# The head of a two-layer graph kernel: the attention weights' product moved to the front of the projections

## The chip, the cores and the metric

The kernel runs on one core of one Trainium2 chip. The time is device microseconds of one execution, as the median of several runs; a profile is one further execution, recorded by the hardware. The engines are TensorE (PE, with its weight load PEld), VectorE (DVE), ScalarE (ACT), GpSimd (POOL) and SyncE (SP, which here only issues DMAs). Each engine takes its instructions in program order and waits for others by semaphores.

## What is computed

Two layers over 4096 rows x of 512 numbers and a 4096 x 4096 matrix adj. Only the start of layer 0 matters here:

```
h = max(layernorm(x), 0)
q = h @ Wq.T + bq ;  k = h @ Wk.T + bk ;  v = h @ Wv.T + bv
x = x + softmax(q @ k.T / sqrt(512) + 2 * adj) @ v
# layer 1: a graph attention with 8 heads over the same rows, W, a1, a2, a_ln, b_ln
```

The kernel never forms k. Since q @ k.T is (h @ Wq.T + bq) @ (h @ Wk.T).T up to a term that is constant along a softmax row, it forms A = Wq.T @ Wk once (512 x 512) and a vector c from bq and Wk, and then "queries" h @ A + c, which are multiplied with h itself. All of it is in fp32.

## The kernel before

`fast_path` does everything (a general path follows for inputs that it can't take; it isn't run here). Its first part, the projections, is what the change touches. Rows come in eight blocks `sb` of 512. These steps exist for a block:

- `load_x(sb)` (L400): four DMAs of 128 rows, 256 KB each, on SP's queue.
- layernorm: `means`/`stats` (L176, L419) take mean and variance on DVE; an inverse root follows; then the rows are scaled and shifted in place. For block 0 `normalize` (L406) does roots and scaling on DVE; for the others `normalize_ahead` (L424) does the roots on POOL and the scaling on ACT (L433).
- `hidden(sb, xt)` (L438): 16 PE transposes (128 x 128) into four PSUM banks `pt`, four ACT relu copies into `hT` (L444), four POOL sums and differences of its quarters into `hS` (L452 to L455), and seven DMAs on SP that store both to DRAM.
- `values_of(sb, between)` (L517): h @ Wv.T + bv by seven half-size products in place of eight (a Strassen scheme, `seven`, L489). The products come in four stages; a stage's results go into PSUM banks named X and Z, two of each, and DVE adds each one into the result (L510, L520). A later product may accumulate on a bank that DVE has read. After each stage, `between` gives one piece of other work to put into the engines' queues. Four POOL differences for each pair of 128-row blocks (L531 to L534) and two stores end it.
- `queries(sb, between)` (L543): the same for h @ A + c. The result tile `qs` has one buffer; four POOL differences (L565 to L568) and seven stores to `q_d` follow.

`seven` needs differences of the quarters of a weight matrix; `weight_sums` (L462) makes them with four POOL instructions, for Wv and for A.

All instructions in this part are under `keep_in_program_order`, so the order in each engine's queue is the order of the code. Before the change it is: loads of x(0), Wv and x(1); loads of Wq and Wk in blocks of 32 columns with 512-byte rows (`load_blocks`, L329) and of Wk once more as whole rows (`wk_rows`); `normalize(x(0))`; Wv's sums; `hidden(0)`; `values_of(0)`, with block 1's statistics and scaling between its stages; four DVE transposes of Wq's 32 x 32 blocks (`turn_blocks`, L337); `hidden(1)`; a POOL multiply of Wk's rows with bq (L611); `values_of(1)` with Wk's four DVE transposes between its stages; c (L615); block 2's statistics and scaling; `attention_vectors` (L210, DVE, for layer 1); the product A (L623, 16 matmuls of 128 x 512 columns, each two PE instructions) and its four ACT copies out of PSUM (L627); A's sums; `queries(0)`; `hidden(2)`; `queries(1)`; then for each further block `values_of`, `hidden` of the next, `queries`. The small preparations for layer 1 (`aside`: constants, centred and weighted W) are cut into steps; `go_on` puts one step in, and stands between stages of `queries(0)` and of the later blocks.

The weights are kept for this time in parts of the big tile `v` whose own values come much later: blocks 8 to 11 and 16 to 31. The bias vectors and layer 1's vectors are loaded from ACT's queue after `hidden(0)`.

Of the kernel before, what the change touches and what calls it, by code (L numbers as in the profile page):

```python
# [10 lines left out]
F32 = mybir.dt.float32  # L11
# [7 lines left out]
P = 128  # L19
# [60 lines left out]
def fast_path(  # L80
# [95 lines left out]
    def means(pool, rows, name, mv=None, some=range(SB)):  # L176

        st = pool.tile([P, SB, 6], F32, name=f"{name}st", tag=f"{name}st", bufs=2)
        if mv is None:
            mv = pool.tile([P, SB, 2], F32, name=f"{name}mv", tag=f"{name}mv", bufs=2)  # L180
        for b in some:
            seq(nc.vector.bn_stats(st[:, b, :], rows[b]))
            seq(nc.vector.bn_aggr(mv[:, b, :], st[:, b, :]))
        return mv
# [11 lines left out]
    def over_heads(t):  # L196
        return t.unsqueeze(1).to_broadcast([P, NH, HD])
# [122 lines left out]
    with tc.tile_pool(name="rows_in", bufs=2) as rows_in, tc.tile_pool(  # L320
# [70 lines left out]
        with tc.tile_pool(name="proj_v", bufs=1) as pv, tc.tile_pool(  # L391
# [11 lines left out]
                    seq(nc.sync.dma_start(out=xt[:, b, :], in_=x[ts(sb * SB + b, P), :]))  # L403
                return xt

            def normalize(xt):  # L406
                mv = means(work, [xt[:, b, :] for b in range(SB)], "h")
                var = work.tile([P, SB], F32, name="hv", tag="hv", bufs=1)
                seq(nc.vector.tensor_scalar_add(var, mv[:, :, 1], LN_EPS))
                rstd = inverse_root(nc.vector, work, var, SB, "h")  # L410
                for b in range(SB):
                    seq(nc.vector.tensor_scalar(
                        xt[:, b, :], xt[:, b, :], mv[:, b, 0:1], rstd[:, b : b + 1],
                        ALU.subtract, ALU.mult,
                    ))

            mvs = {}

            def stats(sb, *blocks):  # L419
# [1 line left out]
                    mvs[sb] = work.tile([P, SB, 2], F32, name="hmv", tag="hmv", bufs=2)  # L421
                means(work, [xts[sb][:, b, :] for b in range(SB)], "h", mvs[sb], blocks)

            def normalize_ahead(sb):  # L424
                mv = mvs.pop(sb)
                var = work.tile([P, SB], F32, name="hv", tag="hv", bufs=1)
                seq(nc.gpsimd.tensor_scalar_add(var, mv[:, :, 1], LN_EPS))
                rstd = inverse_root(nc.gpsimd, work, var, SB, "h")
                shift = work.tile([P, SB], F32, name="hs", tag="hs", bufs=1)
                seq(nc.gpsimd.tensor_mul(shift, mv[:, :, 0], rstd))  # L430
                seq(nc.gpsimd.tensor_scalar_mul(shift, shift, -1.0))
                for b in range(SB):
                    seq(nc.scalar.activation(  # L433
                        xts[sb][:, b, :], xts[sb][:, b, :], AF.Identity,
                        scale=rstd[:, b : b + 1], bias=shift[:, b : b + 1],
                    ))

            def hidden(sb, xt):  # L438
                h, sums = hidden_tiles(sb)
# [134 lines left out]
            def room(first, blocks, m):  # L574
                return v[:, first : first + blocks, :].rearrange(
                    "p b d -> p (b d)"
                ).rearrange("p (m c) -> p m c", m=m)

            raw = {"q": room(16, KC, GC // R), "k": room(20, KC, GC // R)}
# [20 lines left out]
            def turn_weights(name, c):  # L600
                turn_blocks(turned[name][:, c, :], raw[name], c)

            def calls(f, *each):
                return [lambda a=a: f(*a) for a in each]
# [6 lines left out]
            seq(nc.gpsimd.tensor_mul(  # L611
                wk_rows, wk_rows, bq_sb.unsqueeze(1).to_broadcast([P, KC, D])
            ))
            values_of(1, calls(turn_weights, *(("k", c) for c in range(SB))))
            seq(nc.vector.tensor_reduce(c_sb, wk_rows, AX.X, ALU.add))  # L615
            seq(nc.vector.tensor_scalar_mul(c_sb, c_sb, half_scale))
            stats(2, *range(SB))
            normalize_ahead(2)
            attention_vectors(v[:, 15, :])
            for k in range(KC):  # L620
                pa_ps = psum.tile([P, 512], F32, name="pa", tag="XZ"[k % 2], bufs=2)
                for c in range(SB):
                    seq(nc.tensor.matmul(  # L623
                        pa_ps, turned["q"][:, c, ts(k, P)], turned["k"][:, c, :],
                        start=c == 0, stop=c == SB - 1,
                    ))
                seq(nc.scalar.activation(a_sb[:, k, :], pa_ps, AF.Identity, scale=half_scale))  # L627
# [1315 lines left out]
```

## Time and profile before

| | us |
|---|---|
| median of three runs (lowest, highest) | 3564.26 (3562.43, 3565.39) |
| the profiled execution's own time | 3564.05 |
| its span, first to last instruction | 3562.1 |
| PE busy in the span | 3496.1 (98%) |
| DVE, ACT, POOL busy | 2571.6, 1765.6, 2286.7 |
| PE's first instruction | 14.17 |
| first matmul of `values_of(2)` | 95.83 |
| first attention product (L715) | 250.35 |

The projections take the first 250 us. The busy times of a pipelined PE say that it had work, not that it ran at its best, so they are read beside the granted clock (1.00 is full speed). A wait in the views is written with the engine and line that released it: `[2.34 <-ACT a_sb L627]` means that the engine had been idle for 2.34 us until the instruction of line 627 on ACT was done.

### The profile page before, as it was taken

The page shows a single profiled execution, that of the slowest core. Times are in us where ns is not written, and L with a number is a line of the kernel's source. Part 1 is how long each engine was busy: PE and PEld are TensorE (multiplying, and loading weights), DVE is VectorE, ACT ScalarE, POOL GpSimd, SP SyncE. Part 2 cuts the span into 40 slices and gives each one's busy share as a digit, 9 for nine tenths or more (in the row PEclk, how much of TensorE's full clock was granted, in tenths as well). Part 3 has the DMA queues.
Part 4 walks back from the last instruction along what each step waited for, and adds up shares of the span by engine and source line. Part 5 has one row for each costly group of instructions (what it writes and reads, how often), then busy time and mean ns, then how long its engine had stood idle before and what let it go on. Part 6 is the DMA issues. An engine that isn't in the chain of part 4 may idle for free.

```text
span 3562.1 us, 59727 instructions
## 1 busy us (share of the span) xinstructions
PE 3496.1 (98%) x21866; PEld 2149.3 (60%) x21866; DVE 2571.6 (72%) x4268; ACT 1765.6 (50%) x1570; POOL 2286.7 (64%) x1857
## 2 busy tenths in 40 slices
PE   7999999999999999999999999999999999999998
PEld 5888888888888888888878222222322222232222
DVE  5666565656566665656557888888888888888887
ACT  1111111111111111111123899999999999999997
POOL 5664444454444454444456788888888888888886
PEclk9999999999999999999999999999999999999999
DMA  6687888888888788888758777787787777777775
GB/s 204 207 250 226 242 240 236 247 245 236 246 241 242 238 242 246 240 244 240 232 123 182 205 200 205 207 218 207 209 220 215 208 215 205 200 211 208 214 212 151
DMA packets 636958, 779.86 MB, mean 219 GB/s; under 512 B 78512, under 2 KB 465264, under 8 KB 627440
## 3 DMA queue, kind: packets, MB, share of 16 engines
q1 hardware_dynamic: 618800, 742.60, 72.4%
q0 software_dynamic: 16464, 31.98, 5.2%
q8 instruction: 174, 2.85, 0.3%
q10 hardware_dynamic: 1392, 1.38, 0.2%
q14 instruction: 128, 1.05, 0.1%
HBM read 593.76 MB, written 174.19 MB: 216 GB/s over the span
## 4 chain that ended last, share of the span: by engine, by line
PE 88%; DVE 7%; ACT 1%; DMA 1%; issue 1%; POOL 0%; SPq 0%; DVEq 0%; ACTq 0%; POOLq 0%
PE accs L1083 25%; PE XZ L715 21%; PE M L770 20%; PE r L1044 4%; PE r L1014 4%; PE l L1024 3%; PE X L503 3%; PE l L1044 3%; PE Z L503 2%; DVE t L1071 2%; PE y L1276 1%; PE pt L1147 1%; DVE x L826 1%; DVE y L1160 1%; PE accs L1276 1%
## 5 line engine op out<-in xcount | busy, mean ns | idle before, releaser
L1068 POOL TENSOR_TENSOR t<-t,g 128x1024 f32<-128x1024 f32 x512 | 1224.7, 2400 | 272.7 <-DVE t L1062 236.5
L1083 PE MATMUL accs<-t,nX 128*64 128x512 f32 x4096 | 1003.0, 605 | 4.7 <-DVE ob L1137 4.7
L1075 ACT ACTIVATE t<-t 128x2048 f32<-128x2048 f32 (+1 forms) x527 | 976.3, 1853 | 0.2 <-POOL t L1068 0.2
L1062 DVE SCALAR_TENSOR_TENSOR t<-u,at2m,r 128x512 f32<-128x512 f32 x1024 | 719.3, 744 | 193.8 <-issue 151.7
L731 ACT ACTIVATE aT<-aT 128x512 f32<-128x512 f32 x256 | 161.2, 630 | 1388.6 <-DVE aT L727 1388.6
L727 DVE TENSOR_TENSOR aT<-aT,XZ 128x256 f32<-128x256 f32 x891 | 351.5, 418 | 580.6 <-PE XZ L715 576.2
L1071 DVE TENSOR_TENSOR t<-l,g 128x1024 f32<-128x1024 f32 x512 | 623.6, 1218 | 0.0
L1030 ACT ACTIVATE l<-l 128x1024 f32<-128x1024 f32 x512 | 516.3, 1008 | 117.1 <-PE l L1024 65.9
L1083 PEld LDWEIGHTS accs<-t,nX 128*64 128x64 f32 x4096 | 246.4, 136 | 462.5 <-issue 449.7
L715 PE MATMUL XZ<-qt,hS 128*128 128x256 f32 x2040 | 482.8, 379 | 1.0
L715 PEld LDWEIGHTS XZ<-qt,hS 128*128 128x128 f32 x2040 | 387.0, 190 | 56.1 <-DVE aT L727 3.8
L743 POOL TENSOR_TENSOR S<-aT 128x256 f32<-128x256 f32 x128 | 93.0, 727 | 507.3 <-ACT aT L731 507.3
L715 PE MATMUL XZ<-qt,hT 128*128 128x256 f32 x1532 | 372.5, 379 | 2.1 <-DVE aT L727 2.1
L755 POOL TENSOR_TENSOR total<-total,aT 128x256 f32<-128x256 f32 x360 | 325.3, 917 | 9.4
L715 PEld LDWEIGHTS XZ<-qt,hT 128*128 128x128 f32 x1532 | 291.0, 190 | 42.0 <-DVE aT L727 2.5
L1014 PEld LDWEIGHTS <-z 6*128 6x128 bf16 x2048 | 52.4, 91 | 422.2 <-DVE t L1062 353.8
L744 POOL TENSOR_TENSOR aT<-aT 128x256 f32<-128x256 f32 x128 | 93.2, 728 | 284.6 <-ACT aT L731 284.6
L770 PE MATMUL M<-v,aT 128*128 128x256 f32 x1024 | 262.8, 379 | 0.0
L770 PE MATMUL M<-tv,aT 128*128 128x256 f32 x1024 | 262.6, 379 | 0.0
L770 PE MATMUL M<-v,S 128*128 128x256 f32 x1024 | 243.8, 381 | 0.0
L707 DVE SCALAR_TENSOR_TENSOR gs<-ng,aT 128x512 f32<-128x512 bf16 x254 | 224.1, 882 | 8.7
L770 PEld LDWEIGHTS M<-tv,aT 128*128 128x128 f32 x1024 | 194.6, 190 | 26.5
(253 smaller groups left out, 4528.3 us busy)
## 6 DMA issues: line engine op xcount, KB each, us to landing
g<-gT_d SPq DMA_DIRECT2D x128, 1024.0 KB
ag<-in_adj_dram SPq DMA_DIRECT2D x256, 256.0 KB
hS<-s_d SPq DMA_DIRECT2D x64, 1024.0 KB
gT_d<-gs SPq DMA_DIRECT2D x256, 256.0 KB
nb<-nT_d SPq DMA_DIRECT2D x128, 512.0 KB
nx<-nT_d SPq DMA_DIRECT2D x256, 256.0 KB
hT<-h_d SPq DMA_DIRECT2D x64, 768.0 KB
tv<-vt_d SPq DMA_DIRECT2D x128, 384.0 KB
```

Of the source, the lines that this page charges most:

```text
L707: seq(nc.vector.scalar_tensor_tensor(gs, ng, G_MASKED / NEG_BIG, aT, ALU.mult, ALU.add))
L715: seq(nc.tensor.matmul(out, a, b, start=start and k == 0, stop=k == 1, skip_group_check=not start,))
L727: seq(nc.vector.tensor_add(p, before, part))
L755: seq(nc.gpsimd.tensor_add(t, t, a))
L770: seq(nc.tensor.matmul(sums[ic][i][:, u, :], a[:, ts(u, P)], b, start=jt == 0 and u == 0, stop=jt == NB - 2, skip_group_check=u == 1,))
L1030: seq(nc.scalar.activation(lefts[n], lefts[n], AF.Relu, scale=4.0))
L1044: seq(nc.tensor.matmul(out[first + 2 * r][ts(c, HD), :], ident_b[rows, rows], masks[r != c][rows, jt % JB, :], start=False, stop=True, ski ...
L1062: seq(nc.vector.scalar_tensor_tensor(t[:, 2 + e, :], u4[:, e, :], at2m[:, jt, h : h + 1], right[e], ALU.max, ALU.add))
L1068: seq(nc.gpsimd.tensor_mul(t[:, 2:4, :], t[:, 2:4, :], both_heads(n)))
L1071: seq(nc.vector.tensor_mul(logits[n][:, 0:2, :], lefts.pop(n), both_heads(n)))
L1075: seq(nc.scalar.activation(t, t, AF.Exp))
L1083: seq(nc.tensor.matmul(accs[ts(e, HD), hf, :], nX[jt // SB][:, jt % SB, hg * HG + 2 * hf + e, :], t[:, hf + 2 * e, :], start=jt == 0, stop ...
```

## The change

The order of the head becomes: loads of Wq and Wk as whole rows, alternating, 128 rows at a time; then x(0), Wv, bv (now on SP's queue) and x(1). As each 128-row block lands PE turns it with four transposes, and ACT (Wq) or DVE (Wk) copies the result out of PSUM. The 16 matmuls of A follow, with all four result banks open at once and the contraction outermost. Block 0's statistics, roots and scaling go to DVE, POOL and ACT; block 1's statistics follow; then A's copies out of PSUM, Wv's sums, block 1's roots, `hidden(0)`, block 1's scaling, and `values_of(0)` with nothing between its stages, `hidden(1)`, A's sums, the vector c (its multiply now on DVE), `values_of(1)` with block 2's statistics and scaling between, `queries(0)` with `attention_vectors` in four pieces between, `hidden(2)`, `queries(1)`. The second load of Wk goes; c is made in place in Wk's rows. `queries(1)` writes its `qs` into the room of the turned Wq. The aside steps that stood in `queries(0)` go to the later `values_of`, one more in each.

```diff
@@ attention_vectors: two yields in each half but the last
             seq(nc.vector.tensor_mul(prod, aa[e], over_heads(bln2_sb)))
+            yield
             seq(nc.vector.tensor_reduce(at_b[:, e, :], prod, AX.X, ALU.add))
             seq(nc.vector.tensor_mul(aa[e], aa[e], over_heads(aln_sb)))
+            if e == 0:
+                yield
...
-            def normalize(xt):
...
-            def normalize_ahead(sb):
+            def roots(sb):
                 mv = mvs.pop(sb)
...
+                of_rows[sb] = rstd, shift
+
+            def scale(sb):
+                rstd, shift = of_rows.pop(sb)
                 for b in range(SB):
                     seq(nc.scalar.activation(
                         xts[sb][:, b, :], xts[sb][:, b, :], AF.Identity,
                         scale=rstd[:, b : b + 1], bias=shift[:, b : b + 1],
                     ))
...
+            def normalize_ahead(sb):
+                roots(sb)
+                scale(sb)
...
             def queries(sb, between):
-                qs = pc.tile([P, KC, GC], F32, name="qs", tag="qs", bufs=1)
+                qs = v[:, 24:28, :]
+                if sb != 1:
+                    qs = pc.tile([P, KC, GC], F32, name="qs", tag="qs", bufs=1)
...
+            raw = {"q": v[:, 16:20, :], "k": v[:, 20:24, :]}
             turned = {"q": v[:, 24:28, :], "k": v[:, 28:32, :]}
-            wk_rows, bq_sb = v[:, 8:12, :], v[:, 14, :]
-
+            wk_rows, bq_sb = raw["k"], v[:, 14, :]
+
+            for k in range(KC):
+                for name, w in (("q", wqT), ("k", wkT)):
+                    seq(nc.sync.dma_start(out=raw[name][:, k, :], in_=w[ts(k, P), :]))
             xts = {0: load_x(0)}
             for k in range(KC):
                 seq(nc.sync.dma_start(out=wv_sb[:, k, :], in_=wvT[ts(k, P), :]))
+            seq(nc.sync.dma_start(out=bv_sb, in_=bv[None, :].to_broadcast([P, D])))
             xts[1] = load_x(1)
-            load_blocks(raw["q"], wqT)
-            load_blocks(raw["k"], wkT)
-            seq(nc.sync.dma_start(out=wk_rows, in_=wkT.rearrange("(k p) o -> p k o", p=P)))
-            normalize(xts[0])
+            def turn_weights(name, k, copy):
+                pt = psum.tile([P, 512], F32, name="pw", tag="pt", bufs=4)
+                for c in range(SB):
+                    seq(nc.tensor.transpose(pt[:, ts(c, P)], raw[name][:, k, ts(c, P)], ident))
+                seq(copy(turned[name][:, :, ts(k, P)], pt.rearrange("p (c i) -> p c i", c=SB)))
...
+            pa = [
+                psum.tile([P, 512], F32, name="pa", tag="XZ"[k % 2], bufs=2) for k in range(KC)
+            ]
+            for k in range(KC):
+                turn_weights("q", k, nc.scalar.copy)
+                turn_weights("k", k, nc.vector.tensor_copy)
+            for c in range(SB):
+                for k in range(KC):
+                    seq(nc.tensor.matmul(
+                        pa[k], turned["q"][:, c, ts(k, P)], turned["k"][:, c, :],
+                        start=c == 0, stop=c == SB - 1,
+                    ))
+            stats(0, *range(SB))
+            roots(0)
+            scale(0)
+            stats(1, *range(SB))
+            for k in range(KC):
+                seq(nc.scalar.activation(a_sb[:, k, :], pa[k], AF.Identity, scale=half_scale))
             wv = weight_sums(wv_sb, [
                 pv.tile([P, 2, H], F32, name=f"wvt{e}") for e in range(3)
             ])
+            roots(1)
             hidden(0, xts.pop(0))
+            scale(1)
             xts[2] = load_x(2)
-            seq(nc.scalar.dma_start(out=bv_sb, in_=bv[None, :].to_broadcast([P, D])))
             seq(nc.scalar.dma_start(out=bq_sb, in_=bq[None, :].to_broadcast([P, D])))
             load_vectors()
...
-            values_of(0, calls(stats, (1, 0, 1), (1, 2, 3)) + [lambda: normalize_ahead(1)])
-            for c in range(SB):
-                turn_weights("q", c)
+            values_of(0, None)
             hidden(1, xts.pop(1))
             xts[3] = load_x(3)
...
             wa = weight_sums(a_sb, [
...
             ])
+            seq(nc.vector.tensor_mul(
+                wk_rows, wk_rows, bq_sb.unsqueeze(1).to_broadcast([P, KC, D])
+            ))
+            seq(nc.vector.tensor_reduce(c_sb, wk_rows, AX.X, ALU.add))
+            seq(nc.vector.tensor_scalar_mul(c_sb, c_sb, half_scale))
+            values_of(1, calls(stats, (2, 0, 1), (2, 2, 3)) + [lambda: normalize_ahead(2)])
+            vectors = attention_vectors(v[:, 15, :])
...
-            queries(0, [go_on] * 4)
+            queries(0, [lambda: next(vectors, None)] * 4)
...
-                values_of(sb, [lambda: None, lambda: None, go_on, lambda: (go_on(), go_on(), go_on())])
+                values_of(sb, [lambda: None, go_on, go_on, lambda: (go_on(), go_on(), go_on())])
```

More of the change, by code (lines that the diff above doesn't have):

```diff
@@ L404, in load_x @@
                 return xt
-            def normalize(xt):
[L407 to L415, printed above, removed]
             mvs = {}
@@ L436, in normalize_ahead @@
                     ))
+            of_rows = {}
+            def normalize_ahead(sb):
+                roots(sb)
+                scale(sb)
             def hidden(sb, xt):
@@ L572, in queries @@
                     ))
[L574 to L579, printed above, removed]
+            raw = {"q": v[:, 16:20, :], "k": v[:, 20:24, :]}
             turned = {"q": v[:, 24:28, :], "k": v[:, 28:32, :]}
-            wk_rows, bq_sb = v[:, 8:12, :], v[:, 14, :]
+            wk_rows, bq_sb = raw["k"], v[:, 14, :]
+            for k in range(KC):
+                for name, w in (("q", wqT), ("k", wkT)):
+                    seq(nc.sync.dma_start(out=raw[name][:, k, :], in_=w[ts(k, P), :]))
             xts = {0: load_x(0)}
@@ L585, in fast_path, with calls @@
                 seq(nc.sync.dma_start(out=wv_sb[:, k, :], in_=wvT[ts(k, P), :]))
+            seq(nc.sync.dma_start(out=bv_sb, in_=bv[None, :].to_broadcast([P, D])))
             xts[1] = load_x(1)
-            load_blocks(raw["q"], wqT)
-            load_blocks(raw["k"], wkT)
-            seq(nc.sync.dma_start(out=wk_rows, in_=wkT.rearrange("(k p) o -> p k o", p=P)))
-            normalize(xts[0])
+            def turn_weights(name, k, copy):
[3 more added lines that the diff above has]
+                seq(copy(turned[name][:, :, ts(k, P)], pt.rearrange("p (c i) -> p c i", c=SB)))
+            def calls(f, *each):
+                return [lambda a=a: f(*a) for a in each]
+            pa = [
[16 more added lines that the diff above has]
+                seq(nc.scalar.activation(a_sb[:, k, :], pa[k], AF.Identity, scale=half_scale))
             wv = weight_sums(wv_sb, [
@@ L593, in fast_path @@
             ])
+            roots(1)
             hidden(0, xts.pop(0))
+            scale(1)
             xts[2] = load_x(2)
-            seq(nc.scalar.dma_start(out=bv_sb, in_=bv[None, :].to_broadcast([P, D])))
             seq(nc.scalar.dma_start(out=bq_sb, in_=bq[None, :].to_broadcast([P, D])))
             load_vectors()
[L600 to L604, printed above, removed]
-            values_of(0, calls(stats, (1, 0, 1), (1, 2, 3)) + [lambda: normalize_ahead(1)])
-            for c in range(SB):
-                turn_weights("q", c)
+            values_of(0, None)
             hidden(1, xts.pop(1))
             xts[3] = load_x(3)
[L611 to L627, printed above, removed]
             wa = weight_sums(a_sb, [
@@ L651, in ahead_of @@
                 ]
-            queries(0, [go_on] * 4)
+            queries(0, [lambda: next(vectors, None)] * 4)
+            assert next(vectors, None) is None
             hidden(2, xts.pop(2))
```

## Prediction, on record before the result

> **What bounds the kernel now.** I read the page first: slices of the span by engine.
>
> ```profile
> PE   7999999999999999999999999999999999999998
> ```
>
> Each digit is a fortieth, 89 us. TensorE (PE) is at nine tenths or more in every slice but the first and last, so only the head can give anything. Second, the busy time by stage; I put the borders where the timeline shows a stage's first PE instruction. Columns: length, then busy us of PE, its weight load, VectorE (DVE), ScalarE (ACT), GpSimd (POOL), the granted clock, DMA share, GB/s.
>
> ```profile
> core 0: us, PE busy (x) PEld busy (x) DVE busy (x) ACT busy (x) POOL busy (x), PEclk, DMA share, GB/s
> 0.00:14.20 14.20, 0.00 (x0) 0.03 (x1) 9.11 (x20) 1.28 (x1) 6.72 (x11) 1.00 0.93 262
> 14.20:18.35 4.15, 4.14 (x16) 3.14 (x17) 1.22 (x3) 1.79 (x3) 0.00 (x0) 1.00 0.51 113
> 18.35:31.40 13.05, 12.84 (x56) 10.39 (x56) 7.81 (x21) 0.60 (x1) 7.43 (x12) 1.00 0.80 163
> 31.40:36.83 5.43, 3.33 (x17) 2.52 (x17) 2.82 (x5) 4.61 (x7) 5.12 (x9) 0.84 1.10 325
> 36.83:49.83 13.00, 13.00 (x57) 11.12 (x57) 7.01 (x16) 0.60 (x1) 12.22 (x10) 0.94 1.05 383
> 49.83:63.73 13.90, 13.90 (x33) 5.89 (x32) 11.23 (x21) 2.08 (x3) 7.74 (x13) 1.00 0.56 198
> 63.73:66.07 2.34, 0.00 (x1) 0.00 (x1) 0.00 (x0) 2.34 (x6) 0.46 (x1) 0.95 0.00 0
> 66.07:79.81 13.74, 13.74 (x57) 11.79 (x58) 7.05 (x20) 0.43 (x1) 4.57 (x4) 0.88 0.02 5
> 81.55:95.83 14.28, 12.36 (x59) 10.56 (x58) 7.93 (x20) 1.01 (x3) 9.03 (x8) 1.00 0.70 241
> 95.83:110.00 14.17, 14.17 (x75) 12.65 (x74) 8.84 (x26) 4.39 (x8) 11.75 (x18) 1.00 0.54 178
> ```
>
> The rows are: before the first transpose; hidden(0); values(0); hidden(1); values(1); the weights' product; a hole; queries(0); queries(1) (hidden(2), 79.81 to 81.55, not shown); and the start of values(2), where PE is full and stays so (144 of 144 us from 96 to 240). What these stages need at full speed: a hidden stage is 16 transposes, 1.75 us as a piece of the chain of waits; the chain has four PE instructions of a block of seven products as 0.86 us, so the 56 of a block are 12.1 us; the product is 32 instructions, 13.9 us. Three hidden, four blocks, one product: 5.25 + 48.4 + 13.9 = 67.55 us. values(2) starts at 95.83, so **28.3 us of the head is not full-speed PE work**: 14.2 before the first transpose, 2.4 in hidden(0), 0.95 in values(0), 3.7 around hidden(1), 0.9 in values(1), 2.34 in the hole, 1.6 in queries(0), 2.2 in queries(1).
>
> Third, the timeline for what ended those waits (start, length, then the idle time before and its releaser).
>
> ```profile
> 3.49 0.69 DVE L182 BATCH_NORM_STATS2 hst<-xt 128x6 f32<-128x512 f32 x1 [2.55 <-DMA xt<-in_x_dram]
> ...
> 5.59 0.69 DVE L182 BATCH_NORM_STATS2 hst<-xt 128x6 f32<-128x512 f32 x1 [0.39 <-DMA xt<-in_x_dram]
> ...
> 64.48 2.03 ACT L627 ACTIVATE a_sb<-pa 128x512 f32<-128x512 f32 x4
> ...
> 66.07 2.08 PE L503 MATMUL Z<-hT,a_sb 128*128 128x256 f32 x4 [2.34 <-ACT a_sb L627]
> ...
> 86.55 0.48 DVE L552 TENSOR_SCALAR qs<-Z,c_sb 128x256 f32<-128x256 f32 x1 [4.65 <-DMA q_d<-qs]
> ```
>
> PE begins only after x has landed, and after DVE's statistics and scaling. The hole is the product's copies out of PSUM. In queries(1) DVE waits for a store of `qs`, which has one buffer. The clock column adds a second loss: 0.84, 0.94 and 0.88 are spells of half clock, 35.0 to 38.4 (mean 0.51) and about 65.9 to 69.2, each after a sparse stretch.
>
> [...] both spells last about 3.4 us. [...] in hidden(0) ACT's copies follow each other at 0.86 us for four transposes (half clock), and the matmuls right behind them, from 19.4, run at 0.215 us each (full). So I count transposes as warming. [...] the adds out of PSUM here are 0.42 us for 256 columns.
>
> **The change, part by part.**
>
> *Weights first.* Eight loads of 256 KB with 2 KB rows now stand where x and wv stood. The same form, count and place, so the same timing:
>
> ```profile
> GB/s 0 0 0 0 0 0 0 115 66 279 393 377 426 344 172 213 188 205 393 369 393 377 352 230 311 328 336 311 369 418 393 336 361 393 410 402 418 402 401 402
> ```
>
> Slots of 0.25 us. Summed, 2.10 MB (eight loads) is reached by 8.45 us. The lag to use: block 0 (0.26 MB at 2.87) was used at 3.49, block 2 (0.79 MB at 4.73) at 5.59, so 0.6 to 0.9; the last weight block is usable at about 9.2. First transposes at 3.5. Added on PE: 32 transposes, 3.5 us at full and 6.9 at half clock, under loads that last 5.7 us. At half clock the eight groups would end by 10.4, at full clock by 9.7. Then the last copy: DVE PSUM to SBUF, 512 columns. The trace has no such row; 0.60 (ACT, same size) to 0.69 (DVE over 512 columns of fp32); I take 0.66, [...]. **The product starts at about 10.8** (10.5 to 11.6). Removed: eight DVE transposes of 0.70, the eight 512-byte-row loads (8.6 + 3.8 us of SP's issue time) and the second 1 MB load of Wk; DVE and SP had room, so nothing by itself.
>
> *x(0), wv, bv, x(1) behind the weights on SP.* 5.5 MB at about 0.4 MB/us ends near 17, x(0) near 11.8, wv near 14.4. DVE statistics(0): 4 x 0.8, done 14; POOL roots 3.1 (28.37 to 31.47 of before), 17; ACT scales 2.9, 20. The wv sums on POOL 4 x 1.26, 22; roots(1) 25. All lie beside the 13.9 us product (10.8 to 24.7): cost nothing. Without that cover x would come 4.5 us later than now. statistics(1) moves off values(0).
>
> *Copies of the product.* Four ACT copies of 0.58; the banks finish 0.86 apart, so the last ends 0.7 after PE, while hidden(0)'s transposes run. ACT's first relu waits for it: 0.35 us late, about what values(0) pays now. The hole (2.34) and its half-clock spell go.
>
> *Second rows.* hidden(1) finds them scaled (ACT about 27.5 to 30.5, needed near 39): the 3.7 us and the 0.9 of half clock go.
>
> *values(1).* On POOL the sums of the attention weights (5.0) and roots(2) (3.1) now stand behind hidden(1)'s sums, ahead of the values' differences; those sums are ready by 13.4 us after values(0) ends, and queries(0) starts 14.4 after. On DVE the bias vector (the 128x2048 multiply that POOL did in 4.5, at 2.2 like the reduction beside it; that reduction, 2.24; 0.26) stands ahead of the first result: 4.7 us, to 5.2 after values(0). The first bank is wanted again at about 5.3 after. DVE then also has statistics(2), 3.2; following each bank through I find 0.5 us of waiting. The bound: 0.3 to 3 if the order on DVE or POOL slips.
>
> *queries(0).* The attention vectors (4.9 us in all: 0.4 + 3 x 0.69, twice, + 0.2) now stand between stages; 14 results at 0.48 are 6.7, together 11.6 of 12.1. Each step of 1.1 to 1.5 us must fit in a stage's slack of 1.5, and a bank is wanted only a stage later: 0.2 us, at most 2. Four aside steps move into values(2) to values(7), 0.84 us each under 12.1 us blocks with DVE near 0.7 busy: nothing.
>
> *queries(1).* `qs` in dead weight room: the 2.2 goes.
>
> *Queues.* The loads of bq and the four vectors stay on ACT behind hidden(0), now behind scale(1) too: 5 issues of 0.44 from about 30.5, bv's like load landed 3.6 after its issue, so bq is there by 35, read at 39; ACT's next work is hidden(1)'s relu at 39.5. SP: x(2) still stands behind hidden(0)'s last store, which waits for POOL near 33, and lands near 38, used at 44. w1's loads stand behind values(1)'s differences, near 62 instead of 54; first read by aside steps after values(2). Nothing here is late.
>
> *Clock.* PE works from 3.5 with small holes, so I expect it at full clock by 7 to 10. If the product starts at half clock it costs 1.7 us (3.4 at half): chance a quarter, 0.4.
>
> **Sum.** values(2) starts at 10.8 + 67.55 + 0.4 + 0.5 + 0.2 + 0.4 = 79.85 against 95.83: **16.0 us less**. The rest is PE's own chain, shifted whole. The profiled execution took 3564.05 (span 3562.1 and 1.95 around it): 3548.05. The median of the runs shown is 3564.26, 0.2 above, inside their 3 us spread; I keep **3548.0**.
>
> **Rivals.**
> A, the sum holds within its bounds (3545.5 to 3550.5): 0.66.
> B, a new wait takes part of it: the product cold (1.7), DVE held by the bias vector and statistics(2) in values(1) (3), vectors in queries(0) (2), late weights (1): 3 to 8 us lost, 3551 to 3556. For: DVE at 11.6 of 12.1. Against: banks wanted a stage later. 0.24.
> C, the time is taken back later, by something with its own schedule, or the order does not do what it says: 3557 to 3571. Against: from 96 on PE waits for DVE and POOL results of its own products, and the loads follow the work. About 3564; 0.06.
> D, slower: the clock stays at half after the thin start. Each us of full-speed work in it costs one us more; it decides from 16 + 7 = 23 us of such work, and if all 67.55 us of the head ran so the kernel would take 3616. For: PE starts on thin, DMA-paced transposes. Against: both spells of before last 3.4 us under dense work. 0.04.
>
> About 0.2% (7 us) is what a measurement of this kernel can tell from no change. Faster by more: A and B, 0.90. Within: 0.06. Slower: 0.04. The range, 3545 to 3554, takes A and over half of B.
>
> **What would show it.** The product at about 10.8 to 24.7 at clock 1.00; hidden(0) right behind it; no PE gap over 0.6 us before values(2) at about 80; hidden(1) in 1.75; no wait on a `q_d` store in queries(1). Wrong if the weight blocks land after 11, if PE shows waits on DVE in values(1) or on POOL sums, or if PE idles later where it does not now.

## Result and the profile after

| | before | after |
|---|---|---|
| median of seven runs each (lowest, highest), us | 3564.26 (3562.28, 3566.38) | 3554.75 (3551.78, 3556.43) |
| ratio (95% interval) | | 0.9974 (0.9964 to 0.9983) |
| the profiled execution, us | 3564.05 | 3555.78 |
| its span, us | 3562.1 | 3553.7 |
| first matmul of the product A, us | 49.83 | 11.27 |
| first matmul of `values_of(2)`, us | 95.83 | 81.81 |

The kernel is faster by 0.26%, about 9.5 us. The forecast was 16 us, with a range down to 10.3, so the direction held and the size did not.

The page of the changed kernel, slices by engine: the first slice is now full as well.

```profile
PE   9999999999999999999999999999999999999998
```

The same view by stage as before the change, of the changed kernel. The columns are length, busy us of PE, its weight load, DVE, ACT, POOL, then the granted clock, DMA share and GB/s. In order: the weights' transposes; the product; values(0); hidden(1); values(1); queries(0); queries(1); and 20 us around the change from projections to attention. hidden(0) and hidden(2) are left out.

```profile
3.67:11.27 7.60, 6.51 (x32) 5.50 (x33) 2.82 (x5) 2.35 (x4) 0.00 (x0) 1.00 1.00 346
11.27:25.27 14.00, 14.00 (x34) 6.30 (x35) 6.16 (x16) 4.72 (x7) 9.54 (x18) 1.00 0.47 167
...
27.43:39.67 12.24, 12.24 (x56) 10.60 (x57) 5.50 (x13) 3.23 (x5) 7.27 (x8) 1.00 0.81 261
39.67:41.94 2.27, 1.92 (x18) 1.67 (x16) 2.07 (x2) 1.63 (x4) 2.27 (x2) 1.00 0.80 296
41.94:55.89 13.95, 12.78 (x57) 10.49 (x57) 11.39 (x24) 0.44 (x1) 13.46 (x13) 1.00 0.66 211
55.89:67.98 12.09, 12.09 (x58) 10.59 (x57) 9.33 (x20) 2.93 (x4) 8.63 (x15) 1.00 0.34 127
...
69.72:81.81 12.09, 12.09 (x58) 10.64 (x57) 9.80 (x21) 0.96 (x2) 9.45 (x8) 1.00 0.90 310
...
240.00:260.00 20.00, 16.25 (x64) 13.54 (x63) 8.49 (x19) 1.69 (x3) 5.81 (x8) 0.83 0.69 244
```

Nearly every row of the head is what was forecast: the product at 14.00 and full clock, hidden(0) right behind it (25.27), values(0), queries(0) and queries(1) at their full-speed lengths, the hole and the `q_d` wait gone. Three rows are not. hidden(1) takes 2.27 where 1.75 was forecast, since PE still waits 0.35 for ACT's last relu copy. values(1) takes 13.95 where it should take 12.1 and a little. And at 240 to 260, where nothing was changed, PE is busy for only 16.25 of 20 us, at a mean clock of 0.83; the kernel before had 17.36 of 20 at 1.00 in the same stretch, which holds its own change to attention.

To see where the gain stays or goes, I count PE's instructions from the end of both traces (the programs are the same from values(2) on, but for a few instructions on other engines) and subtract the starts of the same instruction. The difference is called the lead of the changed kernel. It is 14.01 us in values(2), 13.76 at the first attention product (236.59 against 250.35), **9.44** at 310, 9.26 at 1700, and 8.78 at the last instruction. So 2 of the forecast 16 us were missing in the head, 4.3 were handed back within 15 us at the change to attention, and the remaining 3,200 us took 0.7.

The chain of waits at the change to attention shows the place, first in the kernel before, then in the changed one (start, length, what).

```profile
251.75 1.29 POOL ts L566
...
253.44 2.42 DMA q_d<-qs
...
255.99 0.44 DVE ng L705
```

```profile
237.98 1.30 POOL ts L570
...
239.67 4.11 DMA q_d<-qs
...
243.91 0.44 DVE ng L714
```

Both chains are the same: the last queries' differences on POOL, the store of the queries that SP issues behind them, and on DVE the first layer-1 mask `ng`, which waits for that store. (No data passes from the store to the mask. The attention's tiles are opened where the projections' tiles are given up, so the wait is presumably for the room; that wasn't tried.) The sums that PE needs (`aT`, L727 before and L736 after) are queued on DVE behind the mask. Only the store's own time differs: 2.42 us before, 4.11 after. PE's timeline has the consequence, first in the kernel before, then in the changed one:

```profile
257.86 1.13 PE L715 MATMUL XZ<-qt,hT 128*128 128x256 f32 x4 [2.06 <-DVE aT L727]
```

```profile
245.78 2.07 PE L724 MATMUL XZ<-qt,hT 128*128 128x256 f32 x4 [3.75 <-DVE aT L736]
247.65 1.91 PE L779 MATMUL M<-v,aT 128*128 128x256 f32 x4
```

In the kernel before, that wait is 2.06, and the four matmuls then take 1.13 us. In the changed one it is 3.75 and they take 2.07: the clock is at half from 244.40 to 251.22. It is not a new wait but an old one that has grown, and a clock that falls behind it.

### The profile page after: what moved, and what is told of

Read it like the earlier page. It is cut to its first block, busy times and chain, and to the rows that moved or that the text cites. A ratio compares the mean times of both kernels' runs of the same rounds, so it can differ in the third digit from the quotient of the medians.

```text
span 3553.7 us, 59795 instructions
## 1 busy us (share of the span) xinstructions
PE 3500.3 (98%) x21898; PEld 2153.7 (61%) x21898; DVE 2572.2 (72%) x4256; ACT 1770.7 (50%) x1578; POOL 2284.5 (64%) x1863
## 4 chain that ended last, share of the span: by engine, by line
PE 90%; DVE 7%; ACT 1%; DMA 1%; issue 1%; POOL 0%; SPq 0%; DVEq 0%; ACTq 0%; POOLq 0%
PE accs L1092 25%; PE XZ L724 21%; PE M L779 21%; PE r L1053 4%; PE r L1023 4%; PE l L1033 3%; PE X L505 3%; PE l L1053 3%; PE Z L505 2%; DVE t L1080 2%; PE y L1285 1%; PE pt L1156 1%; DVE x L835 1%; DVE y L1169 1%; PE accs L1285 1%
## 5 line engine op out<-in xcount | busy, mean ns | idle before, releaser
L736 DVE TENSOR_TENSOR aT<-aT,XZ 128x256 f32<-128x256 f32 x891 | 351.5, 418 | 581.0 <-PE XZ L724 576.6
L779 PEld LDWEIGHTS M<-v,aT 128*128 128x128 f32 x1024 | 195.1, 191 | 26.7
```

What stands on the lines that cost most here:

```text
L736: seq(nc.vector.tensor_add(p, before, part))
L779: seq(nc.tensor.matmul(sums[ic][i][:, u, :], a[:, ts(u, P)], b, start=jt == 0 and u == 0, stop=jt == NB - 2, skip_group_check=u == 1,))
```

## The experiments

Theory H: the head delivers some 14 to 16 us, and part is handed back at the change to attention, by the wait for the last queries' store and by time at half clock behind it; the head itself falls short by POOL's late sums in values(1) and by a late start of the product. Rival S: the shortfall is spread over the run, by no single place. Rival W: it is all the thin, cold start. An edit that is worth a microsecond or two is near the scatter of the runs, so each experiment is read twice: in its profile, at the place concerned, and in its median. A result is given as the median in us (lowest to highest), then the ratio to the kernel before on the same chip (95% interval).

**The same kernel again.**

> The changed kernel itself, profiled and timed once more beside the next three. Theory H (handed back): the head gains 14 us and a wait of PE at the change-over to the attention (the first product after stage 2, behind DVE's mask of block 2, which waits for the store of the last queries) gives 2 to 4.4 back, by its own length and by the half clock that follows it. Then this profile has that wait again, 2 to 4 us, and the total is 3552 to 3556; where the wait is shorter the half-clock spell is too. Rival S (spread): the changed kernel is slower by a few us all along, or the median is a matter of which runs were drawn; then the 14 us of the head shrink evenly over the span, and the change-over has no special part.

3552.76 (3550.13 to 3554.54), ratio 0.9967 (0.9955 to 0.9980). In its profile the product starts at 10.81 and the lead at the start of attention is 14.2; at the change PE waits 2.15, and one spell of 3.41 us at half clock follows: the lead falls to 12.5. So one and the same program hands back 4.3 us in one execution and 1.7 in another, and H's size is a range, not a number. S falls here and in the first result: the lead is flat from 310 to 1700 in both (9.44 to 9.26; 12.48 to 12.34). But there is a second place where it moves, behind 1700, where layer 0 changes to layer 1 and every profile has spells at half clock: here it falls from 12.34 to 10.48 by the last instruction. Over the eleven profiles of the changed head that part brings anything from 1.9 lost to 1.7 won. It wasn't followed further; it is one more reason why a median answers so weakly to an edit in front of it.

**The masks moved behind the sums that PE needs** (the first pair's two `for_layer_1` steps after its last stage), in the changed kernel and in the one before:

```diff
-            for n, (f, s) in enumerate(((swap, 2), (for_layer_1, 2), (swap, 3), (for_layer_1, 3))):
-                stage(0, n, w)
-                f(s)
+            for n, s in enumerate((2, 3, None, None)):
+                stage(0, n, w)
+                if s:
+                    swap(s)
+            for s in (2, 3):
+                for_layer_1(s)
```

> The changed kernel with the two mask steps of DVE (blocks 2 and 3, for layer 1) put behind stage 3 of the first attention pair, so that no add of stage 2 stands behind the wait for the store. H: the wait of PE falls from 3.75 to under 1 us and the half clock of 6.8 us after it goes: 3.0 + 2.6, less what still lags, 4 to 5.5 us faster than the changed kernel, 3549 to 3551. S: no more than 1 us, 3554.

> The kernel before with the same edit. There the wait is 2.06 us and no half clock follows it. H: 1 to 2 us faster than before, 3562 to 3563, so that between this and the changed kernel with the same edit nearly the whole gain of the head, 12.5 to 14 us, is left. S: no change, and a distance of 9 to 10 us as without the edit.

The changed kernel with it: 3552.56 (3547.66 to 3553.43), 0.9964 (0.9951 to 0.9978). In its profile the wait for `aT` is 0.51, another of 0.92 comes for a load of `tv`, there is no half clock, and the lead is kept whole (12.3 to 12.5). But its product started only at 12.78, so it entered with less, and the median is no better than that of the unedited kernel. The kernel before with it: 3563.65, 0.9996 (0.9988 to 1.0005); its lead over the unedited one rises by 0.6 at the place, no more, since in the unedited one the wait was only 2.06 and the clock stayed up. The profile bears H out; both medians miss what H had expected (3549 to 3551, and 3562 to 3563).

**The vector c out of values(1)** (multiply, reduction and scaling on DVE behind block 1's statistics; bq's load on SP behind bv):

```diff
             stats(1, *range(SB))
+            seq(nc.vector.tensor_mul(
+                wk_rows, wk_rows, bq_sb.unsqueeze(1).to_broadcast([P, KC, D])
+            ))
+            seq(nc.vector.tensor_reduce(c_sb, wk_rows, AX.X, ALU.add))
+            seq(nc.vector.tensor_scalar_mul(c_sb, c_sb, half_scale))
```

> The changed kernel with the bias vector c made on DVE right behind block 1's statistics, while the product runs, and bq loaded on SP behind bv for it. H: the first POOL difference of values(0), 2.81 us beside DVE's 128x2048 multiply instead of 0.73, is back at 0.73; the waits of PE for POOL's sums in values(1), 0.95 and 0.22 us, shrink to under 0.4, and values(2) starts 1.0 to 1.5 us earlier, near 80.6. Rival: POOL is late in values(1) because of the order of its queue; then the difference is still slow or the sums still late, and values(2) stays at 81.8. The total moves by 0.5 to 1.5 us, unless the change-over hides it.

3550.70 (3547.46 to 3554.51), 0.9960 (0.9946 to 0.9974). In values(1) of the changed kernel the timelines of DVE, POOL and PE had read:

```profile
40.22 2.28 DVE L633 TENSOR_TENSOR v<-v 128x2048 f32<-128x2048 f32 x1
```

```profile
40.27 2.81 POOL L533 TENSOR_TENSOR tv<-v 128x256 f32<-128x256 f32 x1
43.05 0.72 POOL L534 TENSOR_TENSOR tv<-v 128x256 f32<-128x256 f32 x1
```

```profile
46.66 1.13 PE L505 MATMUL Z<-wvt,hS 128*128 128x256 f32 x4 [0.95 <-POOL hS L454]
48.02 1.13 PE L505 MATMUL X<-wv_sb,hS 128*128 128x256 f32 x4 [0.22 <-POOL hS L455]
```

With c moved, POOL's same instruction:

```profile
40.33 0.73 POOL L533 TENSOR_TENSOR tv<-v 128x256 f32<-128x256 f32 x1
```

and PE no longer waits for that sum:

```profile
45.62 1.03 PE L505 MATMUL Z<-wvt,hS 128*128 128x256 f32 x4
```

A POOL difference that takes 0.73 took 2.81 where DVE's 128x2048 multiply starts 0.05 ahead of it: it ends 0.58 after the multiply does (42.50). In all six profiles of the changed head that keep the multiply there (the changed kernel, again, after_late, warm_only, warm_late, fill) the same difference takes 2.81 or 2.82. What the two instructions contend for, no view shows. The edit doesn't remove the meeting but moves it to a place where PE doesn't wait: beside the product the multiply takes 3.18 in place of 2.28, and a POOL sum takes 3.20 where its like takes 1.28 just before.

```profile
20.46 3.18 DVE L616 TENSOR_TENSOR v<-v 128x2048 f32<-128x2048 f32 x1
```

```profile
18.86 1.28 POOL L471 TENSOR_TENSOR wvt<-wv_sb 128x512 f32<-128x512 f32 x1
...
21.57 3.20 POOL L473 TENSOR_TENSOR wvt<-wv_sb 128x512 f32<-128x512 f32 x1
```

All four profiles with c moved have such a POOL sum of 3.20 there, beside a multiply of 2.54 to 3.20. In values(1) of the changed kernel the sums behind the slowed difference come 2.1 later, and PE waits 0.95 and 0.22. With c moved, values(1) takes 12.25 in place of 13.95 (42.00 to 54.25). The 1.7 is more than the two waits of 1.17 together. The edit also took 5.1 us of DVE's work out of values(1), where DVE had been held by c until 45.32, so the remaining 0.5 isn't assigned.

The head can now be put as one number: its lead at the start of attention plus the start of its product. It is 25.01 to 25.04 in the six profiles without this edit that keep the rest of the changed head (again, after_late, warm_only, warm_late, fill and the changed kernel), and 26.70 to 26.72 in the four with it. **c in values(1) costs 1.7 us, every time**; what else differs between the heads of these ten is when the product starts.

**Both, and both with ten PE transposes of the identity in front** (from 1.35 us, ahead of the first weights):

```diff
+            pt = psum.tile([P, 512], F32, name="pw", tag="pt", bufs=4)
+            for n in range(10):
+                seq(nc.tensor.transpose(pt[:, ts(n % SB, P)], ident, ident))
             for k in range(KC):
                 turn_weights("q", k, nc.scalar.copy)
```

> The changed kernel with both edits: the mask steps behind stage 3 and c made early. Theory H (handed back: waits at the change-over, POOL slowed by DVE's multiply in values(1), and steps of 1.7 us for each window of 3.41 us at half clock): values(2) starts 1.2 us earlier than in the changed kernel from the same start of the product, no half clock between the head and the second layer, and the gain that stands at values(2), 15 us, still stands at 1700 us: 3548 to 3550.5. Rival S (the change-over has no part): the gain at 1700 us is again 9 to 12, and the median within 1 us of the early c alone, 3550.7.

> The same with ten transposes of the identity on PE ahead of the first weights; they read and make nothing that is used. H: [...] the clock is full by 8.2 at the latest, in every run, where it came between 7.9 and 12.6 in the profiles so far; the product starts at 10.6 to 11.0 and not up to 12.8: 0.3 to 2 us less than without, 3547 to 3549. If transposes don't count as work for the clock, it comes where it came and nothing changes.

3548.13 (3547.62 to 3551.85), 0.9959 (0.9946 to 0.9973), and 3546.92 (3546.85 to 3549.90), 0.9958 (0.9944 to 0.9971): the best of all versions, 14.5 and 15.7 under the kernel before on their chip, where the forecast had said 16 of the change alone. In the profile of the second, the lead is 15.8 at the start of attention and 16.0 at 310. In the first it falls from 15.1 to 12.8, against what H had expected, by a wait in another place and a spell at half clock behind it (245.32 to 248.73):

```profile
241.20 1.13 PE L724 MATMUL XZ<-qt,hT 128*128 128x256 f32 x4 [0.51 <-DVE aT L736]
...
245.18 1.07 PE L779 MATMUL M<-tv,S 128*128 128x256 f32 x2 [1.99 <-DMA nT_d<-ng]
```

So the edit removes one wait and leaves another, two products on: 0.92 and 1.15 in two of the four profiles with the masks moved, whose lead is kept, 1.99 and 1.97 in the other two, which hand back 2.3 and 1.6.

**Two parts of the change alone.** Block 1's statistics, roots and scaling put back between the stages of `values_of(0)`; and, in the kernel before, only the second room for `qs`:

```diff
-            stats(1, *range(SB))
...
-            roots(1)
...
-            scale(1)
...
-            values_of(0, None)
+            values_of(0, calls(stats, (1, 0, 1), (1, 2, 3)) + [lambda: normalize_ahead(1)])
```

```diff
-                qs = pc.tile([P, KC, GC], F32, name="qs", tag="qs", bufs=1)
+                qs = v[:, 24:28, :]
+                if sb != 1:
+                    qs = pc.tile([P, KC, GC], F32, name="qs", tag="qs", bufs=1)
```

> The changed kernel with block 1's statistics, roots and scaling back in between the stages of values(0), as before: the second half of the change undone. Priced at 3.7 us around hidden(1), and 0.9 more if half clock follows: values(2) at 85 to 86.5 instead of 81.8, total 3 to 5 us over the changed kernel, 3556 to 3558. Rival: ACT and POOL have so much room now that the scaling ends with values(0), and under 1 us is lost.

> The kernel before with the room of the turned Wq for the queries of block 1, the one part alone. H: the 1.92 us wait of PE in queries(1) goes, values(2) starts 2.0 to 2.2 us earlier, 3562. Rival: DVE or POOL takes it up (the four sums wait for the same stores) and less than 0.5 us is won.

after_rows: 3554.81 (3552.60 to 3557.35), 0.9977 (0.9967 to 0.9986), with values(2) starting at 85.27, as expected. hidden(1) waits for ACT's scaling again, and a spell at half clock follows at 44.68:

```profile
41.70 0.33 PE L445 MATMUL pt<-ident,xt 128*128 128x128 f32 x1 [0.96 <-ACT xt L429]
```

before_qs: 3563.65 (3559.42 to 3564.85), 1.0000 (0.9991 to 1.0008). Its lead is 2.6 us in the head. Of this 0.45 is there before queries(1), from an earlier start; the edit's part is the 2.2 that was forecast for it. The lead is 1.0 after the change to attention, where its wait is the old 2.05 but a spell at half clock now follows (256.54 to 259.95). The kernel before, too, can lose a spell there; it had not in the profile that I predicted from.

**What the start is worth, and whether the single edits are worth anything.** The ten transposes alone, with the masks moved, and with c moved, which with the runs above gives every combination of the three edits:

> The changed kernel with ten PE transposes of the identity ahead of the first weights' transposes, nothing else. H (the head's start is a matter of the clock alone, and about 2 to 5 us of the head's gain are handed back at the change-over to attention by the wait for the last queries' store and by half-clock windows after it): clock full by 7.4 to 8.9, product at 10.8 to 11.0, head gain 14.0 to 14.6, change-over wait 2 to 4, one or two windows of 3.41 us at half clock there, time 3551 to 3553. Rival W (the whole shortfall against the forecast is the thin start): time 3548 to 3549 and no loss at the change-over.

> As warm_only, with the two for_layer_1 steps of the first pair moved behind its last stage, so that no mask stands on DVE ahead of the sums that PE waits for. H: head gain 14.0 to 14.6 and all of it kept over the change-over (wait 0.5 to 1.5, no half clock), 2 to 4 us better than warm_only: 3548.5 to 3550.5. Rival L (the order of the masks is worth nothing, since the store is waited for elsewhere): within 1 us of warm_only.

> As warm_only, with the vector c made on DVE after the second block's statistics in place of the time of values(1), and its bias loaded on SP behind bv. H: the head is 1.2 us better than warm_only (gain 15.4 to 16.0, no wait for a POOL sum in values(1)), and the change-over takes 2 to 5 of it as in warm_only: 3549.5 to 3552. Rival P (POOL's slow sums are hidden anyway): same as warm_only.

| median us (runs) | neither | masks moved | c moved | both |
|---|---|---|---|---|
| without the ten transposes | 3552.76 (6) | 3552.56 (5) | 3550.70 (5) | 3548.13 (5) |
| with them | 3552.68 (6) | 3552.33 (6) | 3552.89 (5) | 3546.92 (5) |

The cells come from three chips. The kernel before took 3564.12 on that of the first three cells of the first line, 3564.29 on that of the first three of the second, and 3562.63 on that of both "both" cells, so these two may look 1 to 1.5 better than they are. The ratios of the three new ones are 0.9967 (0.9955 to 0.9979), 0.9966 (0.9954 to 0.9978) and 0.9964 (0.9950 to 0.9978). Of my expectations, the time of warm_only held, though its product came at 11.4; those of warm_late and warm_c missed, as both are no faster than warm_only. The profile of warm_late loses 0.6 of its lead at the wait of 1.97 and 1.0 more at 271.25, again for a load of `tv`; that of warm_c starts its product at 12.38 and hands back 3.7. One cell says little, since the runs of one program lie 3 to 7 us apart. All 43 runs together, each less the mean of the kernel before on its chip, by least squares with an effect for each edit: c moved 1.6 us faster (plus or minus 1.2), masks moved 1.5 (1.2), the ten transposes 0.1 (1.2). The first agrees with the 1.7 of the profiles. Whether the two help more together than apart isn't settled (1.3 more, plus or minus 2.4; both "both" cells share one chip). W falls, though not by this edit: the product ran at full clock in every profile, and its late start is worth 0.7 on the average. The transposes bring full clock at 6.0 to 10.8 in place of 7.9 to 12.6 (that it would be full by 8.2 in every run was an estimate; in warm_c it came at 10.8), but the product still starts at 10.8 to 12.4 (11.4 on the average, against 11.6 without them), because the second block of Wq lands as late as before: PE waited 0.17 to 1.43 for it. Where that wait was the same, 1.02 to 1.04, the product came at 11.41 with the transposes, and at 12.08 and 12.78 without: they help a little, and the scatter of the loads hides it.

**The gap filled.** 24 PE transposes of the identity, whose results nobody reads, ahead of the first pair's last stage:

```diff
+                if n == 3:
+                    pf = psum.tile([P, 512], F32, name="pf", tag="M1", bufs=1)
+                    for u in range(24):
+                        seq(nc.tensor.transpose(pf[:, ts(u % SB, P)], ident, ident))
                 stage(0, n, w)
                 f(s)
```

> The changed kernel with 24 PE transposes of the identity (about 2.6 us at full clock, results read by nobody) put into PE's queue ahead of the first pair's last stage, where PE waits for DVE's sum. They do not shorten the wait; they keep the array busy in it. H (part of what is handed back is the half-clock windows that follow the gap): wait up to 1.5 left, no half clock in 244 to 252, and 2 to 4 us handed back in place of 1.7 to 4.4: 3550.5 to 3553. Rival G (the wait alone counts, the clock does not): windows at half clock remain or their absence changes nothing: 3552 to 3555, as the changed kernel, or later if the transposes outlast the wait.

```profile
242.69 2.78 PE L884 MATMUL pf<-ident 128*128 128x128 f32 x24
245.50 1.13 PE L724 MATMUL XZ<-qt,hT 128*128 128x256 f32 x4
...
248.10 0.67 PE L779 MATMUL M<-tv,S 128*128 128x256 f32 x2 [0.60 <-DMA tv<-vt_d]
```

3552.64 (3550.60 to 3554.45), 0.9966 (0.9954 to 0.9978). The matmuls come no earlier than the mask lets them (1.87 after the mask's start at 243.63, as in the changed kernel), but they run at 1.13 and no half clock follows. 1.4 us are handed back, the least of all profiles of the changed head with the masks in their old place. That is one execution, and the kernel before had one without a spell too. In the median it can't be told from the unedited kernel, and the ranges of H and G overlap there.

**The account of the change to attention.** If what is handed back is the wait beyond the 2.06 of before, plus half of the time that PE then works at half clock, it must add up in every profile with the old order of masks and nothing put into the gap:

| profile | wait | half clock after it | sum | measured |
|---|---|---|---|---|
| changed kernel | 3.75 | 5.44 | 1.69 + 2.72 = 4.4 | 4.3 |
| after_c | 4.13 | 5.65 | 2.07 + 2.82 = 4.9 | 4.8 |
| warm_c | 4.13 | 3.41 | 2.07 + 1.71 = 3.8 | 3.7 |
| after_rows | 2.78 | 3.41 | 0.72 + 1.71 = 2.4 | 2.4 |
| warm_only | 2.61 | 3.41 | 0.55 + 1.71 = 2.3 | 2.2 |
| again | 2.15 | 3.41 | 0.09 + 1.71 = 1.8 | 1.7 |
| before_qs | 2.05 | 3.41 | 0 + 1.71 = 1.7 | 1.6 |

It does, within 0.1. The wait itself follows the store's landing. From the mask's start less the store's start, that is 2.55 to 2.64 in three profiles (the kernel before, before_qs, again) and 3.08 to 4.61 in six (the changed kernel, after_c, after_rows, warm_only, warm_c, fill). In the eight of these whose gap wasn't filled, PE's wait is that time less 0.5. In the six, over the stretch from 3 us ahead of the store to the mask, the view of the DMA queues has one packet of the queue that it calls `instruction`, and in the three it has none (the line is from the changed kernel):

```profile
q8 instruction: 1, 0.02, 1.3%
```

This isn't enough to call the packet the cause. A longer wait makes the stretch longer, and so likelier to hold a packet. In warm_only the packet lies ahead of the store: from the store's start at 239.86 on, the view has none. In fill it comes only in the last 0.63 us before the mask. What makes the store long stays open, and so does whether the change makes it likelier: the long ones are six of seven profiles of the changed head, and none of two of the head before.

## Why the prediction was right in direction and wrong in size

- *The product at 10.8 (10.5 to 11.6).* 11.27 in the profiled run, 10.8 to 12.8 over ten profiles with the same or nearly the same start. The weight blocks came later than forecast: I let one early curve of bytes stand for all. In the profiled run the third load's bytes, 0.79 MB in all, had moved by 4.5, but it was used at 5.87, 1.4 later and not 0.6 to 0.9 (in others as late as 6.9); the last block's transposes began at 9.86, where I had it usable at 9.2. Behind them, PE waited 0.78 for the last copy, which took 0.69; my 9.7 to 10.8 left 1.1 for it, an estimate. In the latest of the ten, 12.78, PE also worked at half clock until 12.57. Cost: 0.5 in the profiled run, 0.7 on the average of the ten.
- *The clock at the start, 0.4.* The product ran at full clock throughout, in all ten profiles: the clock rose at 6.0 to 12.6, each time ahead of the product, with nothing but transposes on PE. So in these runs transposes alone brought it up, as read from hidden(0); in the profiled run it took from 3.67, PE's first, to 8.88. My 7 to 10, an estimate, held there.
- *Copies, second rows, qs, queries(0).* Nearly all as forecast: hidden(0) to values(0) lost 0.41, hidden(1) found its rows scaled but took 0.5 longer than the 1.75 forecast, the `q_d` wait is gone. That `bv` loses nothing in SP's queue was an estimate; DVE's first add of it (28.65) waits for PE, where before it had idled 6.52 until the load landed. (In queries(0) the parts of the attention vectors add to 5.1, not 4.9; nothing hung on it.) after_rows takes the second rows' part back: its lead plus product start is 22.5 against 25.0, so in the changed kernel that part is worth 2.5 where I put 4.6 (3.7 and 0.9). before_qs does the last part alone: 2.2, as I put it.
- *values(1), 0.5 us of waiting.* 1.85 over full speed, and 1.7 more than without c there. I counted the queues of DVE and POOL each by itself and named the bound of 3 "if the order slips"; the order held, but a POOL instruction of 0.73 took 2.81 beside DVE's multiply.
- ***"The rest is PE's own chain, shifted whole."*** This is the step that failed. At the change to attention a chain that is not PE's stands ahead of it: POOL, a store, a mask. It was in the trace of before, with 2.06 us of PE idle that end at 257.86, and I had read that chain; but the forecast prices the stages up to 240 and takes what follows to be of fixed length. Being there already, it would have shifted with the rest if its length were fixed; it is not. 1.6 to 4.8 us were handed back in the seven profiles above, 4.3 in the profiled one.
- *The sum.* Of the 16.0, 0.5 goes with the start, 1.35 in values(1) beyond the 0.5 allowed, 0.5 in hidden(1) and 0.25 in values(0) and the product; 0.6 comes back, as the terms for the clock (0.4) and queries(0) (0.2) weren't needed. That is 14.0 at values(2), as measured. Between values(2) and attention 0.25 more goes (near 118 in the profiled run), in every profile of the changed head and in none of the head before; I had put the moved aside steps there at nothing, and what takes it wasn't followed. From 13.76 at the start of attention, less 4.3 and 0.7, it is 8.8 at PE's last instruction, 8.4 in the span and 8.3 in the time of the profiled pair. The medians differ by 9.5, so the profiled run is one that handed back more than most. The repeat of the same kernel, 3552.76, lies inside the range of 3545 to 3554 and the first result, 3554.75, outside it. That is luck of the executions: the step failed in both.
- *The rivals.* B's interval (3551 to 3556) held the time, and its bias vector in values(1) was a real part of it. The larger part was C's mechanism, something with its own schedule, at a size that I had not given it. D is excluded: the half clock ended at 8.9 us, and by 12.6 in every other profile of the changed start. What I had named as a sign of error, that PE idles later where it does not now, was put too narrowly: it idled longer where it idled already.

What stays open: why the store takes 2.4 in some executions and 4.1 in others, what moves the lead behind 1700, and whether moving the masks helps more than its 1.5 us when c is moved too.

## What to carry to other kernels

A saving at the head of a kernel arrives at the end only if every wait on the way moves with it: follow the trace of before through each change of phase, and list the waits there that end on a DMA: here one such store took 2.4 us in one execution and 4.1 in another. Where two engines are filled beside each other, read in a trace whether an instruction takes as long beside the other engine's as alone (here a POOL difference of 0.73 took 2.81), not only whether each queue fits. And where one execution differs from the next by more than an edit can bring, read the edit's place in the profiles, and let all combinations of the edits share their runs.

## What the runs showed of the hardware

The clock moved in steps of 3.41 us. In the changed kernel it rises at 8.88, falls at 244.40, rises at 251.22 and falls at about 1801: 235.52, 6.83 and 1549.65 us, which are 69, 2 and 454 times 3.413. In the kernel before it falls at 35.10 and at 65.82, for 3.41 us each, and stays up for 1740.80 us from 69.23 on, 510 times 3.413. Where the steps lie differs between executions: from 8.88 in the one profile to 35.10 in the other is 7.68 steps, no whole number. The first rise of the changed kernel's second profile is at 8.81, of other profiles with the same start at 7.85 to 12.57.

At the change to attention, no step at half clock followed 2.06 us of idling (the kernel before) and once 1.97 (warm_late); one step each followed 1.99 (late_c), 2.05 (before_qs), 2.15 (again), 2.61 (warm_only) and 2.78 (after_rows), two followed 3.75 (the changed kernel), and 4.13 was followed once by two (after_c) and once by one (warm_c). So at this place the length of the gap alone doesn't decide; what else does, isn't shown. A step at half clock costs up to 1.7 us, half of its length: four matmuls `M<-v,aT` took 1.91 us in it (247.65 in the changed kernel) and 1.03 at full clock (252.87). The two profiles of the changed kernel itself differ by 3.0 us in their lead at 310: 0.5 of it is the start of the product, and 2.6 the store's landing with the half clock behind it.
